# The first 40 microseconds of an attention and FFN block: layer norm's order, its engines, and the queues of the first transfers

## The chip, the cores and the metric

The kernel runs on one core of one Trainium2 chip. Its time is the device time of one execution in microseconds; several executions are taken, and the median counts. A core has five engines that run on their own and meet at semaphores: TensorE (PE, with its weight loads as PEld), VectorE (DVE), ScalarE (ACT), GpSimd (POOL) and SyncE (SP), which here only issues transfers. ACT, POOL and SP can all issue transfers; each works through its instructions in the order of the program.

## The reference

Two sequences of 1024 tokens with 512 features (x is 2 x 1024 x 512, 2048 tokens in all, float32) go through

```python
xn = _layernorm(x)                         # no scale, no shift
s  = attention(xn, w_qkv, b_qkv, w_out, b_out)   # 32 heads of 16, ALiBi, causal softmax
g  = silu(octonion_ffn(xn, w_gate, w_up, w_down)) # weights made ternary: sign times mean |W|
out = x + s * g
```

In the attention, `scores = q k^T / 4 + slope_h * position_k`, masked to the past, softmax, times v, then the output projection. In the FFN each weight is replaced by `scale * clip(round(W / scale), -1, 1)` with `scale = mean |W|` and expanded by the signs of octonion multiplication; `silu(gate) * up` goes through the down weights.

## The kernel before, in words

The tokens are 16 tiles of 128. Eight (the first sequence) are normalised in the head of the kernel, the other eight in the midst of the attention. A tile `t` goes through these steps:

- `measure`: DVE takes mean and variance (`bn_stats`, `bn_aggr`).
- `root`: ACT takes the square root, DVE the reciprocal `rs` and `nb = -mean * rs`.
- `normal`: ACT scales the 128x512 tile in place (`xt`).
- `norm_item`: PE turns the four 128x128 pieces into a PSUM buffer `ptx`, ACT copies them to `xnT` (tokens along the free axis).

In the head `tokens(t)` calls the first three for one tile in a row, so that DVE waits for ACT's root and ACT for DVE's `nb` within each tile.

Heads are worked on in groups of four, and q and k are produced for pairs of groups: `qk_items(b, gp)` are 16 products `pqk` (which of q and k, which half `c` of the tokens, four steps `kt`). A product of 512 columns shows as two PE instructions ("passes"). A finished `pqk` is biased by ACT and DVE into a staging tile `st` of two float32r parts, which SP writes to DRAM (`sp<-st`). `fill_k` and `fill_q` read it back into stacks `k_stack`, `q_stack`, which hold 64 rows of heads, two rows of ALiBi (`al_dram`, made by `alibi_parts`) and two rows for the negated maximum. One half of a stack is four transfers of 128 KB on SP, for k one more from `al_dram`.

Attention runs in 32 units (sequence, group, half of the queries). For each unit PE first makes scores for the row maxima, DVE reduces them (`max_items`), PE and ACT turn the maxima and POOL's queue places them in the q stack (`place_max`, `q_stack<-mr`); then the scores are made again with the maximum in them, ACT takes the exp (`exp_step`, `exp_of`), and PE multiplies by v (`value_step`).

The ternary weights are loaded with three transfers each (`load_weight`: `w_g`, `w_u`, `w_d`). `ternary_sum` is a DVE reduction over such a weight, `ternary_total` a small PE product `tot_g` of the sums, `ternary_signs` two DVE passes, and `keep_signs` writes the signs of the gate and up weights to DRAM.

The order of the instructions on every engine is written out when the program is made, and the engines keep it. For the head it is written by hand or in a list of items (`lead_in`). For the attention a planner in the same function chooses the next item: it keeps a clock `now` with costs per item (436 for a tile's turning, 858 for one q/k step, 431 for one v step, in ns), models of when ACT and DVE will be done, when a filled stack will have landed (`fill_at`, with a step `link` for each fill), and when a weight will be there (`known`). `load_later(w, name)` puts a load of a weight behind a time `known["k", name]` and assumes it landed 9000 later (`known["l", name]`); `weight(name)` then puts sum, total and signs behind that. The items of `later` are taken in the order in which they were put. PSUM buffers are few: three for exp scores, two for maxima, one for the values, and two (`ps_m`) for all the rest, the turned tiles, `pqk`, `pv` and placed maxima among them.

In the kernel before, all eight x tiles are loaded on SP's queue, the first q/k weights (`wqr`) on ACT's beside them, the gate weights on POOL's, the up and down weights and all later `wqr` on ACT's; the 16 x 8 biases of q and k come with eight transfers on SP. The ALiBi table `al_sb` and its low part share the pool of the staging tiles `st`, which has two buffers. 20 products on ones (`idle`, 40 passes) run on PE while nothing else can.

Of the kernel before, what the change touches and what calls it, by code (L numbers as in the profile page):

```python
# [75 lines left out]
def kernel(  # L76
# [108 lines left out]
        )  # L185
        wv_tiles[n] = w

    bqk_sb = aw.tile([P, 2, NP], F32, name="bqk_sb")
    bv_sb = aw.tile([P, D], F32, name="bv_sb")
    mask = aw.tile([P, 512], F32, name="mask")  # L190
    bo_sb = aw.tile([P, D], F32, name="bo_sb")
# [9 lines left out]
    def load_x(t, eng):  # L201
# [3 lines left out]
        eng.dma_start(out=xt, in_=x[t * P : (t + 1) * P, :])  # L205
        x_tiles[t] = xt

    warm = wk.tile([64, 1], F32, tag="rs1", name="warm")
    act_.activation(warm, ones[:, 0:1], AF.Sqrt)
    for t in range(8):  # L210
        load_x(t, sp_)
    load_wq((0, 0), act_)
    load_wv(0)
    for n in range(2):
        for i in range(4):
            sp_.dma_start(
                out=bqk_sb[n * 64 + i * HD : n * 64 + (i + 1) * HD, :, :],
                in_=bqk[i * 32 : i * 32 + HD, :].rearrange(
                    "d (w g n) -> d w g n", w=2, n=2
                )[:, :, :, n],  # L220
            )
    al_sb = stg.tile([P, S], F32, tag="st", name="al_sb")[0:H, :]
    pool_.dma_start(out=al_sb, in_=calibi)
    pool_.dma_start(out=mask, in_=cmask)
    pool_.dma_start(out=bv_sb, in_=bv.partition_broadcast(P))
    add_ring(early, 1, 2)

    xn_tiles = {}
# [9 lines left out]
        dve_.bn_stats(st, x_tiles[t])  # L238
        dve_.bn_aggr(mv[:, t % n, :], st)

    def root(t, n):

        mv = moments[t]
        sd = wk.tile([P, n], F32, tag=f"sd{n}", name=f"sd_{t}")
        act_.activation(sd, mv[:, :, 1], AF.Sqrt, bias=eps)
        rs = wk.tile([P, n], F32, tag=f"rs{n}", name=f"rs_{t}")
        dve_.reciprocal(rs, sd)
        nb = wk.tile([P, n], F32, tag=f"nb{n}", name=f"nb_{t}")
        dve_.scalar_tensor_tensor(nb, mv[:, :, 0], -1.0, rs, ALU.mult, ALU.mult)
        moments[t] = rs, nb  # L250

    def normal(t, n):
        rs, nb = moments[t // n * n]
        i = t % n
        xt = x_tiles.pop(t)
        act_.activation(
            xt, xt, AF.Identity, bias=nb[:, i : i + 1], scale=rs[:, i : i + 1]
        )
        xn_tiles[t] = xt


# [112 lines left out]
    def alibi_parts():  # L374

        for n in range(2):
            home, tag = (stg, "st") if n else (wop, "wo")
            part = home.tile([P, S], F32R, tag=tag, name=f"al_{n}")[0:H, :]
            if n == 0:
                dve_.tensor_copy(part, al_sb)  # L380
                high = part
            else:
                dve_.tensor_tensor(part, al_sb, high.bitcast(F32), ALU.subtract)
            sp_.dma_start(out=al_dram[n], in_=part.bitcast(F32))

    def norm_item(t):
# [64 lines left out]
    def qk_items(b, gp):  # L451

        box = {}

        def product(which, c, kt):
            if (which, c, kt) == (0, 0, 0):
                if (b, gp) not in wq_tiles:
                    compact_wq((b, gp))
                parts[b, gp] = [
                    spill.tile([2, P, S], F32, tag=f"sp{w}", name=f"sp_{b}_{gp}_{w}")  # L460
                    for w in range(2)
                ]
# [3 lines left out]
            pe(  # L466
                nc.tensor.matmul(  # L467
                    ps,
                    lhsT=wq_tiles[b, gp][:, kt, which, :],
                    rhs=xnT[:, kt, b * S + c * 512 : b * S + (c + 1) * 512],  # L470
                    start=(kt == 0),
                    stop=(kt == KD - 1),
                )
            )
            n = b * NP + gp + 1
            if (which, c, kt) == (1, n > 1, KD - 1) and n < B * NP:
                load_wq((n // NP, n % NP), act_)
            if kt < KD - 1:
                return
            bias = bqk_sb[:, which, gp : gp + 1]  # L480
# [353 lines left out]
    def unit_of(lst, n):  # L834
        return lst[n][0] if n < len(lst) else NU
# [78 lines left out]

    def load_later(w, name):
        later(
            lambda: load_weight(w, name, act_),
            lambda: set_known(("l", name), now[0] + 9000),
            ("k", name),
        )  # L920
# [24 lines left out]
    def more_tokens(t0):  # L945

        for t in range(t0, t0 + 4):
            later(
                lambda t=t: measure(t, 4),
                lambda t=t: set_known(("m", t), run_dve(max(now[0], known["x"]), 900)),  # L950
                "x",
            )
            begin[0] += 0.2
        later(
            lambda: root(t0, 4),
            lambda: run_dve(run_act(known["m", t0 + 3], 2800), 350),
        )
# [15 lines left out]
    for n in range(20):  # L973
        pe(nc.tensor.matmul(idle[:, 0:P], lhsT=ones, rhs=ones, start=True, stop=True))
    qk, vs = qk_items(0, 0), v_items(0, 0)
    def tokens(t):
        measure(t, 1)
        root(t, 1)
        normal(t, 1)

    def norm_of(t):
        put([(436, lambda: norm_item(t), "t", ("n", t))])

    make_mask()
    compact_wq((0, 0))
    add_ring(early, 1, 0)
    make_signs()
    load_weight(wg, "g", pool_)
    known.update({("n", t): 7500 + 1600 * t for t in range(8)})
    known.update({("l", "g"): 40000})  # L990
    tokens(0)
    tokens(1)
    for t in range(4):
        norm_of(t)
        quick(lambda t=t: tokens(t + 2))
    put(qk[0:4])
    quick(lambda: (tokens(6), tokens(7), alibi_parts()))
    put(qk[8:12])
    for t in range(4, 8):
        norm_of(t)  # L1000
    put(qk[4:8] + qk[12:16])
    quick(lambda: (begin_v(0, 0), compact_wq((0, 1)), add_ring(early, 2, 3)))
    due = [int(size[0] * n / len(vs)) for n in range(len(vs))]
    lead_in += [(d // 4, None, it) for d, it in zip(due, vs)]
    head_v = len(lead_in)
    lead_in += [(size[0] + 4 * d, None, it) for d, it in zip(due[::2], qk_items(0, 1))]
    known["k", "u"] = 25000
    load_later(wu, "u")
    weight("g")
    later(lambda: keep_signs(0, "g"))  # L1010
# [21 lines left out]
    begin[0] = 10  # L1032
    later(load_wo)
    side = [(d, ok or (lambda: True), it) for d, ok, it in lead_in + side]
    done_qk = [0]

# [9 lines left out]
    SOON = 80  # L1046
    RUN = 1800
    HELD = 1e12
    now, kind = [0.0], ["F"]
    act, dve = [0.0], [0.0]  # L1050
    e_free, x_free, m_free = [0.0] * 3, [0.0] * 2, [0.0] * 2
    o_free = [0.0]
# [18 lines left out]
        dve[0] = max(dve[0], t) + cost  # L1071
        return dve[0]

    qk_done = []

    def try_fill():

        n, part = divmod(fills[0], 4)
        if n >= B * NG or len(qk_done) <= (n // 2 + 1 if n > 1 else part // 2):
            return  # L1080
        if unit_of(exps, E[0]) < 2 * (n - 2) + (0, 1, 2, 2)[part]:
            return
        (fill_q if part % 2 else fill_k)(n // NG, n % NG, part // 2)
        fills[0] += 1
        link[0] = max(now[0], link[0], qk_done[n // 2 + 1 if n > 1 else part // 2]) + 4500
        fill_at.append(link[0] + 2500)

    def try_fetch():
# [114 lines left out]
    def next_side(pos):  # L1203
# [6 lines left out]
        def go():  # L1210
# [345 lines left out]
```

## Time and profile before

| what | value |
|---|---|
| median of 3 runs | 1130.24 us (1127.89 to 1131.73) |
| the profiled execution | 1131.04 us |
| its span, first to last instruction | 1129.2 us |
| mean granted TensorE clock | 0.979 |
| busy: PE / DVE / ACT / POOL | 94% / 61% / 45% / 15% |
| SP's queue: packets, bytes | 66336, 87.48 MB |
| ACT's queue | 3552, 9.78 MB |
| POOL's queue | 3776, 5.98 MB |

A page of the profile gives the busy time of each engine, the span in slices, the DMA queues, and the costliest groups of instructions. A timeline lists instructions in the order of time, merged where the same ones follow each other: start, duration, engine, line, operation, output and inputs, count, and in brackets the idle time of the engine before it with what ended it. "PE ... [3.98 <-ACT xnT]" says that PE did nothing for 3.98 us and that ACT's copy to xnT released it. Names of engines with a q (SPq, ACTq) are of their sequencers, which issue transfers. Line 69 is a helper that issues nearly all instructions of ACT, DVE, POOL and SP, so these go by the tiles' names. The granted clock is the share of full speed that TensorE was given; the records start some 20 us into the span, and a stretch without one is shown as 1.00.

### The profile page before, as it was taken

What the parts mean: (1) busy time and instruction counts of PE and PEld (TensorE: products, weight loads), DVE (VectorE), ACT (ScalarE), POOL (GpSimd) and SP (SyncE); (2) the same over time, 40 slices, a digit from 0 to 9 for tenths busy, and PEclk for the clock granted to TensorE, in tenths of its full rate; (3) what the DMA queues carried; (4) which work ended last, traced back from release to release, by engine and by line L of the source; (5) the groups of instructions that cost most, each with busy time, mean ns of one, the idle gap of its engine ahead of it and who ended that gap; (6) DMA issues with size and microseconds to landing.
All of it is one profiled execution on the core that took longest, in us unless ns stands there. A gap on an engine that the chain in (4) does not pass through costs nothing. (4 is left out here: it accounts for less than half of the span.)

```text
span 1129.2 us, 15583 instructions
## 1 busy us (share of the span) xinstructions
PE 1060.6 (94%) x5562; PEld 700.6 (62%) x5562; DVE 684.5 (61%) x1405; ACT 506.6 (45%) x962; POOL 171.8 (15%) x289
## 2 busy tenths in 40 slices
PE   7879978999999999999999999999899999999995
PEld 5644545675656666556566565665456678878784
DVE  5367786867677777777777867777842114141313
ACT  4122647663844635446445364464583123232322
POOL 6401013010111010100101000001002123242322
PEclk9889979999999999999999999999999999999998
DMA  6886463444735416353442443831131123030110
GB/s 197 202 146 147 99 170 95 67 63 118 151 85 124 101 34 107 135 100 63 122 83 41 103 87 97 139 72 48 43 105 61 47 66 112 1 103 10 58 54 37
DMA packets 73740, 104.24 MB, mean 92 GB/s; under 512 B 26992, under 2 KB 31120, under 8 KB 73664
## 3 DMA queue, kind: packets, MB, share of 16 engines
q1 hardware_dynamic: 66336, 87.48, 34.0%
q10 hardware_dynamic: 3552, 9.78, 2.8%
q0 software_dynamic: 3776, 5.98, 2.1%
q8 instruction: 45, 0.74, 0.3%
q14 instruction: 31, 0.25, 0.1%
HBM read 69.58 MB, written 33.10 MB: 91 GB/s over the span
## 5 line engine op out<-in xcount | busy, mean ns | idle before, releaser
L69 ACT ACTIVATE p<-s 128x512 f32<-128x512 f32 x576 | 310.0, 601 | 125.2 <-PE s L654 70.3
L538 PE MATMUL s<-k_stack,q_stack 126*128 126x512 f32 (+3 forms) x768 | 278.9, 417 | 23.6 <-DVE mx L69 16.1
L654 PE MATMUL s<-q_stack,k_stack 128*128 128x512 f32 (+3 forms) x768 | 229.5, 367 | 13.6 <-DMA q_stack<-mr 8.4
L69 DVE TENSOR_REDUCE mx<-s 128x1 f32<-128x384 f32 (+3 forms) x352 | 226.0, 642 | 11.7
L69 DVE TENSOR_REDUCE left<-s 128x1 f32<-128x512 f32 x256 | 169.1, 685 | 77.0 <-PE s L538 76.0
L538 PEld LDWEIGHTS s<-k_stack,q_stack 126*128 126x128 f32 x768 | 133.1, 194 | 119.0 <-PE s L538 38.4
L654 PEld LDWEIGHTS s<-q_stack,k_stack 128*128 128x128 f32 x768 | 140.3, 193 | 62.2 <-ACT p L69 20.0
L69 DVE TENSOR_TENSOR s<-s,mask 128x128 f32<-128x128 f32 (+2 forms) x352 | 123.9, 352 | 39.4 <-PE s L538 37.7
L692 PE MATMUL po<-p,v 128*32 128x512 f32 (+3 forms) x1536 | 139.0, 490 | 0.3 <-ACT p L69 0.3
L467 PE MATMUL pqk<-xnT,wq 128*128 128x512 f32 x256 | 128.4, 609 | 3.9 <-ACT xnT L69 2.0
L69 DVE SCALAR_TENSOR_TENSOR h<-pu,sc_u,sg 128x512 f32<-128x512 f32 (+1 forms) x44 | 33.0, 750 | 157.9 <-PE pu L1375 153.1
L69 POOL DMA_DIRECT2D q_stack<-mr x64 | 32.1, 507 | 606.5 <-ACT mr L69 606.5
L673 PE MATMUL s<-mask_r,ident_r 128*128 128x256 f32 (+1 forms) x320 | 89.6, 280 | 0.0
L69 POOL TENSOR_TENSOR hs<-h,hs 128x512 fp32r<-128x512 f32 (+1 forms) x43 | 56.2, 1307 | 206.9 <-ACT hs L69 206.9
L692 PEld LDWEIGHTS po<-p,v 128*32 128x32 f32 x1536 | 42.7, 109 | 72.0 <-issue 69.2
L69 ACT ACTIVATE sg<-pg,sc_g 128x512 f32<-128x512 f32 (+1 forms) x44 | 30.4, 691 | 99.7 <-PE pg L1375 99.7
L69 ACT ACTIVATE st<-pqk,bqk_sb 128x512 fp32r<-128x512 f32 x32 | 22.1, 691 | 117.1 <-PE pqk L467 108.7
L425 PE MATMUL pv<-wv,xnT 128*128 128x256 f32 x256 | 68.4, 385 | 1.9 <-DVE v L69 1.5
L467 PEld LDWEIGHTS pqk<-xnT,wq 128*128 128x128 f32 x256 | 47.7, 195 | 31.7 <-issue 21.1
L69 ACT CAST hs<-h 128x512 fp32r<-128x512 f32 (+1 forms) x44 | 27.3, 621 | 85.3 <-DVE h L69 85.3
L673 PEld LDWEIGHTS s<-mask_r,ident_r 128*128 128x128 f32 x320 | 61.3, 192 | 2.1
L761 PE MATMUL pout<-wo_sb,oT 128*128 128x512 f32 x128 | 61.4, 595 | 0.6 <-ACT oT L69 0.6
(145 smaller groups left out, 1103.1 us busy)
## 6 DMA issues: line engine op xcount, KB each, us to landing
sp<-st SPq DMA_DIRECT2D x32, 512.0 KB
k_stack<-sp SPq DMA_DIRECT2D x128, 128.0 KB
q_stack<-sp SPq DMA_DIRECT2D x128, 128.0 KB
wqr<-in_wqk_dram ACTq DMA_DIRECT2D x16, 512.0 KB
xt<-in_x_dram SPq DMA_DIRECT2D x16, 256.0 KB
att<-o SPq DMA_DIRECT2D x32, 128.0 KB
ot<-att SPq DMA_DIRECT2D x16, 256.0 KB
proj<-y SPq DMA_DIRECT2D x16, 256.0 KB
```

The costliest lines, as they stand in the source:

```text
L69: ins = issue(*args, **kwargs)
L425: nc.tensor.matmul(ps[:, 0:256], lhsT=xnT[:, c, b * S + kt * P : b * S + (kt + 1) * P], rhs=wv_tiles[2 * b + hh][:, c, :], start=(c == 0), ...
L467: nc.tensor.matmul(ps, lhsT=wq_tiles[b, gp][:, kt, which, :], rhs=xnT[:, kt, b * S + c * 512 : b * S + (c + 1) * 512], start=(kt == 0), st ...
L538: nc.tensor.matmul(ps[:, j * n : (j + 1) * n], lhsT=q_of(b, g, qc)[0 : NR - 2, first + j, tl * P : (tl + 1) * P], rhs=k_of(b, g, c)[0 : NR ...
L654: nc.tensor.matmul(ps[:, c0 : c0 + w], lhsT=k_of(b, g, kt // 4)[0:NR, h, kt % 4 * P : (kt % 4 + 1) * P], rhs=q[0:NR, h, 512 - w : 512], st ...
L673: pe(nc.tensor.matmul(out, lhsT=ident_r, rhs=rhs, start=False, stop=True))
L692: nc.tensor.matmul(po[32 * i : 32 * i + 32, 512 - w : 512], lhsT=v[:, kt, h * VC : h * VC + 32], rhs=p[:, i * part + c0 : i * part + c0 + ...
L761: nc.tensor.matmul(ps, lhsT=turned[t][:, c, :], rhs=wo_sb[0][:, c, :], start=(c == 0), stop=(c == KD - 1),)
```

## The change

It rewrites the head and the queues that its transfers use:

- Layer norm in the head: `root` is cut in `deviation` (ACT) and `factors` (DVE), and `first_half(t)` takes the moments of tile t and the factors and scaling of tile t - 1. Every second tile (the odd ones) is scaled by POOL (`tensor_scalar`) in place of ACT. The order of the head's steps, with the first eight q/k products, is written out, with two products on ones (`busy(2)`) behind each of the first four turned tiles.
- Transfers: `wqr` of the first pair stands on SP's queue between x tiles 3 and 4; all later `wqr`, the gate, up and down weights go on SP's queue too. `wv`, the 128 columns of the mask that are read, and `bv` follow on SP behind the ALiBi parts. The gate weights leave POOL's queue for a place in the planner (36000 on its clock, the up weights 46000, before 25000).
- Biases of q and k: two transfers on POOL, with the two halves of the partitions shifted by one column, in place of eight on SP.
- The ALiBi table goes to a buffer of the pool of exp results (`pp`), not of the staging tiles.
- The planner starts at HEAD = 21500 with two q/k products done, and its steps for the first group's fills are 3000 in place of 4500.
- POOL's fills of the further stacks and the sign tables come in another order, before the second pair's weights are compacted.

```diff
-    bqk_sb = aw.tile([P, 2, NP], F32, name="bqk_sb")
+    bqk_sb = aw.tile([P, 2 * NG + 1], F32, name="bqk_sb")
...
-    for t in range(8):
+    for t in range(4):
         load_x(t, sp_)
-    load_wq((0, 0), act_)
-    load_wv(0)
+    load_wq((0, 0), sp_)
+    for t in range(4, 8):
+        load_x(t, sp_)
+
+    al = pp.tile([P, 2, S], F32, tag="p", name="al")[0:H]
+    pool_.dma_start(out=al[:, 0], in_=calibi)
+
     for n in range(2):
-        for i in range(4):
-            sp_.dma_start(
-                out=bqk_sb[n * 64 + i * HD : n * 64 + (i + 1) * HD, :, :],
...
-    al_sb = stg.tile([P, S], F32, tag="st", name="al_sb")[0:H, :]
-    pool_.dma_start(out=al_sb, in_=calibi)
-    pool_.dma_start(out=mask, in_=cmask)
-    pool_.dma_start(out=bv_sb, in_=bv.partition_broadcast(P))
+        pool_.dma_start(
+            out=bqk_sb[n * 64 : n * 64 + 64, 1 - n : 1 - n + 2 * NG],
+            in_=bqk.rearrange("(i d) c -> i d c", d=32)[:, 0:HD, :],
+        )
...
-    def normal(t, n):
+    def normal(t, n, on_pool=False):
...
+        if on_pool:
+            pool_.tensor_scalar(
+                xt, xt, rs[:, i : i + 1], nb[:, i : i + 1], ALU.mult, ALU.add
+            )
...
-            if (which, c, kt) == (1, n > 1, KD - 1) and n < B * NP:
-                load_wq((n // NP, n % NP), act_)
+            if (which, c, kt) == (1, 1, KD - 1) and n < B * NP:
+                load_wq((n // NP, n % NP), sp_)
...
     def load_later(w, name):
         later(
-            lambda: load_weight(w, name, act_),
+            lambda: load_weight(w, name, sp_),
...
+    def first_half(t):
+        measure(t, 1)
+        deviation(t, 1)
+        if t % 4:
+            factors(t - 1, 1)
+            normal(t - 1, 1, (t - 1) % 2 == 1)
+
+    for t in range(3):
+        first_half(t)
+    norm_item(0)
+    busy(2)
+    first_half(3)
+    norm_item(1)
+    busy(2)
+    compact_wq((0, 0))
+    factors(3, 1)
+    normal(3, 1, True)
+    for t in (2, 3):
+        norm_item(t)
+        busy(2)
     make_mask()
-    compact_wq((0, 0))
+    alibi_parts()
+    load_wv(0)
+    sp_.dma_start(out=mask[:, 384:512], in_=cmask[:, 384:512])
+    sp_.dma_start(out=bv_sb, in_=bv.partition_broadcast(P))
+    for t in range(4, 7):
+        first_half(t)
+    issue(qk[0:4])
+    norm_item(4)
+    first_half(7)
+    norm_item(5)
+    issue(qk[8:12])
+    factors(7, 1)
+    normal(7, 1, True)
+    norm_item(6)
+    norm_item(7)
     add_ring(early, 1, 0)
+    begin_v(0, 0)
+    add_ring(early, 2, 3)
     make_signs()
-    load_weight(wg, "g", pool_)
-    known.update({("n", t): 7500 + 1600 * t for t in range(8)})
-    known.update({("l", "g"): 40000})
...
     put(qk[4:8] + qk[12:16])
-    quick(lambda: (begin_v(0, 0), compact_wq((0, 1)), add_ring(early, 2, 3)))
+    quick(lambda: compact_wq((0, 1)))
...
-    known["k", "u"] = 25000
+    known["k", "g"] = 36000
+    known["k", "u"] = 46000
+    load_later(wg, "g")
     load_later(wu, "u")
...
-    done_qk = [0]
+    done_qk = [2]
+    HEAD = 21500.0
...
-    now, kind = [0.0], ["F"]
+    now, kind = [HEAD], ["F"]
...
-    qk_done = []
+    qk_done = [HEAD + 4500]
...
+        if n == 0 and now[0] < qk_done[part // 2] - 4000:
+            return
...
-        link[0] = max(...) + 4500
+        link[0] = max(...) + (4500 if n else 3000)
...
-                if done_qk[0] == 2 or done_qk[0] % 4 == 0:
+                if done_qk[0] % 4 == 0:
```

More of the change, by code (lines that the diff above doesn't have):

```diff
@@ L209 @@
     act_.activation(warm, ones[:, 0:1], AF.Sqrt)
-    for t in range(8):
+    for t in range(4):
         load_x(t, sp_)
-    load_wq((0, 0), act_)
-    load_wv(0)
-    for n in range(2):
-        for i in range(4):
-            sp_.dma_start(
-                out=bqk_sb[n * 64 + i * HD : n * 64 + (i + 1) * HD, :, :],
[L218 to L221, printed above, removed]
-    al_sb = stg.tile([P, S], F32, tag="st", name="al_sb")[0:H, :]
-    pool_.dma_start(out=al_sb, in_=calibi)
-    pool_.dma_start(out=mask, in_=cmask)
-    pool_.dma_start(out=bv_sb, in_=bv.partition_broadcast(P))
+    load_wq((0, 0), sp_)
[3 more added lines that the diff above has]
+    pool_.dma_start(out=al[:, 0], in_=calibi)
+    for n in range(2):
+        pool_.dma_start(
+            out=bqk_sb[n * 64 : n * 64 + 64, 1 - n : 1 - n + 2 * NG],
+            in_=bqk.rearrange("(i d) c -> i d c", d=32)[:, 0:HD, :],
+        )
     add_ring(early, 1, 2)
@@ L239, in measure, with deviation @@
         dve_.bn_aggr(mv[:, t % n, :], st)
-    def root(t, n):
+    def deviation(t, n):
         mv = moments[t]
@@ L245, in root, with factors @@
         act_.activation(sd, mv[:, :, 1], AF.Sqrt, bias=eps)
+        moments[t] = mv, sd
+    def factors(t, n):
+        mv, sd = moments[t]
         rs = wk.tile([P, n], F32, tag=f"rs{n}", name=f"rs_{t}")
@@ L255, in normal @@
         xt = x_tiles.pop(t)
-        act_.activation(
-            xt, xt, AF.Identity, bias=nb[:, i : i + 1], scale=rs[:, i : i + 1]
-        )
+        if on_pool:
+            pool_.tensor_scalar(
+                xt, xt, rs[:, i : i + 1], nb[:, i : i + 1], ALU.mult, ALU.add
+            )
+        else:
+            act_.activation(
+                xt, xt, AF.Identity, bias=nb[:, i : i + 1], scale=rs[:, i : i + 1]
+            )
         xn_tiles[t] = xt
@@ L376, in alibi_parts @@
         for n in range(2):
-            home, tag = (stg, "st") if n else (wop, "wo")
-            part = home.tile([P, S], F32R, tag=tag, name=f"al_{n}")[0:H, :]
             if n == 0:
-                dve_.tensor_copy(part, al_sb)
+                part = wop.tile([P, S], F32R, tag="wo", name="al_high")[0:H, :]
+                dve_.tensor_copy(part, al[:, 0])
                 high = part
             else:
-                dve_.tensor_tensor(part, al_sb, high.bitcast(F32), ALU.subtract)
+                part = al[:, 1].bitcast(F32R)
+                dve_.tensor_tensor(part, al[:, 0], high.bitcast(F32), ALU.subtract)
             sp_.dma_start(out=al_dram[n], in_=part.bitcast(F32))
@@ L475, in product @@
             n = b * NP + gp + 1
-            if (which, c, kt) == (1, n > 1, KD - 1) and n < B * NP:
-                load_wq((n // NP, n % NP), act_)
+            if (which, c, kt) == (1, 1, KD - 1) and n < B * NP:
+                load_wq((n // NP, n % NP), sp_)
             if kt < KD - 1:
                 return
-            bias = bqk_sb[:, which, gp : gp + 1]
+            bias = bqk_sb[:, 1 + 2 * (which * NP + gp) :][:, 0:1]
             st = stg.tile([P, 2, 512], F32R, tag="st", name=f"st_{b}_{gp}_{which}_{c}")
@@ L954, in more_tokens @@
         later(
-            lambda: root(t0, 4),
+            lambda: (deviation(t0, 4), factors(t0, 4)),
             lambda: run_dve(run_act(known["m", t0 + 3], 2800), 350),
@@ L975, with busy, issue @@
     qk, vs = qk_items(0, 0), v_items(0, 0)
-    def tokens(t):
-        measure(t, 1)
[L978 to L982, printed above, removed]
-    make_mask()
-    compact_wq((0, 0))
+    def busy(n):
+        for _ in range(n):
+            pe(nc.tensor.matmul(idle[:, 0:P], lhsT=ones, rhs=ones, start=True, stop=True))
+    def issue(items):
+        for _, emit, _ in items:
+            emit()
+    def first_half(t):
+        measure(t, 1)
+        deviation(t, 1)
[15 more added lines that the diff above has]
+        busy(2)
+    make_mask()
+    alibi_parts()
[13 more added lines that the diff above has]
+    norm_item(7)
     add_ring(early, 1, 0)
+    begin_v(0, 0)
+    add_ring(early, 2, 3)
     make_signs()
-    load_weight(wg, "g", pool_)
-    known.update({("n", t): 7500 + 1600 * t for t in range(8)})
-    known.update({("l", "g"): 40000})
[L991 to L1000, printed above, removed]
     put(qk[4:8] + qk[12:16])
-    quick(lambda: (begin_v(0, 0), compact_wq((0, 1)), add_ring(early, 2, 3)))
+    quick(lambda: compact_wq((0, 1)))
     due = [int(size[0] * n / len(vs)) for n in range(len(vs))]
@@ L1084, in try_fill @@
         fills[0] += 1
-        link[0] = max(now[0], link[0], qk_done[n // 2 + 1 if n > 1 else part // 2]) + 4500
+        link[0] = max(now[0], link[0], qk_done[n // 2 + 1 if n > 1 else part // 2]) + (4500 if n else 3000)
         fill_at.append(link[0] + 2500)
```

## The prediction

> **What bounds the kernel now.** I read the page first, then busy time by stretches, then the timelines of PE, DVE, ACT and SyncE over the first 160 us, then SP's own waits.
>
> The page, sections 1 and 2:
>
> ```profile
> span 1129.2 us, 15583 instructions
> PE 1060.6 (94%) x5562; PEld 700.6 (62%) x5562; DVE 684.5 (61%) x1405; ACT 506.6 (45%) x962; POOL 171.8 (15%) x289
> ```
>
> TensorE sets the end: 68.6 us of the span are its idle time, and whatever the change gives must come out of these, or out of PE work that brings nothing (the 40 passes on "ones", 8.9 us), or out of work done at half clock. The profiled execution took 1131.0 us (span 1129.2 and 1.8 around it), 0.8 over the median of 1130.24; sums are made against 1131.0 and the 0.8 is taken off at the end.
>
> PE's timeline (start, duration, line, what, count, the idle time before it and who ended it), cut to the head:
>
> ```profile
> 1.08 8.90 PE L974 MATMUL idle<-ones 64*128 64x128 f32 x40 [1.08 <-DVE ones L69]
> 9.90 1.97 PE L391 MATMUL ptx<-ident,xt 128*128 128x128 f32 x8
> ...
> 17.51 8.52 PE L467 MATMUL pqk<-xnT,wq 128*128 128x512 f32 x16 [1.35 <-ACT xnT L69]
> ...
> 30.45 2.80 PE L391 MATMUL ptx<-ident,xt 128*128 128x128 f32 x12 [3.98 <-ACT xnT L69]
> 33.92 8.86 PE L467 MATMUL pqk<-xnT,wq 128*128 128x512 f32 x16 [0.68 <-ACT xnT L69]
> 42.62 7.61 PE L425 MATMUL pv<-wv,xnT 128*128 128x256 f32 x34
> ...
> 57.19 0.38 PE L320 MATMUL tot_g<-wsum_g,ones 64*128 64x1 f32 x2
> ...
> 78.93 0.76 PE L654 MATMUL s<-q_stack,k_stack 128*128 128x512 f32 x1 [3.88 <-DMA q_stack<-mr]
> ```
>
> Two waits stand out: 3.98 us in the head, and 3.88 us ahead of the first exp scores. The cause of the first is on ACT: the second staging tile `st` shared its pool with `al_sb`, and DVE's alibi work came late.
>
> ```profile
> 29.23 0.69 ACT L69 ACTIVATE st<-pqk,bqk_sb 128x512 fp32r<-128x512 f32 x1 [1.07 <-DVE al L69]
> ```
>
> From 42.8 to 78.9 PE was idle 6.2 us (1.54 + 0.41 + 0.33 + 3.88 in its timeline). SyncE's queue in that stretch, and DVE's first use of the gate weights:
>
> ```profile
> 48.37 1.73 SPq L69 DMA_DIRECT2D k_stack<-sp  x4
> ...
> 52.41 2.85 SPq L69 DMA_DIRECT2D k_stack<-sp  x4
> 56.98 3.30 SPq L69 DMA_DIRECT2D q_stack<-sp  x4
> 60.98 3.27 SPq L69 DMA_DIRECT2D k_stack<-sp  x4
> 64.99 0.23 SPq L69 DMA_DIRECT2D k_stack<-al_dram  x1
> 65.95 3.30 SPq L69 DMA_DIRECT2D q_stack<-sp  x4
> 55.26 1.55 DVE L69 TENSOR_REDUCE wsum_g<-w_g 64x1 f32<-64x1360 f32 x1
> ```
>
> Each fill of a quarter stack (128 KB) takes 1.0 us of this queue, because an issue waits for earlier fills to land (SP's waits name k_stack and q_stack DMAs for 15.8 us). From the first fill of half 1 (48.37) to the last of group 1 (68.95) are 20.6 us, and whatever stands behind in SyncE's queue waits for all of them. `w_g` didn't: it went out on GpSimd's queue at 17.1.
>
> **The change, part by part.**
>
> Layer norm of tiles 0 to 3. DVE still starts at 5.44 behind its two memsets; the staggered order has tile 0 scaled at about 8.4 (0.69 + 0.18 and 0.30 for the root, one more stats pair before the factors, 0.82 scaling). But PE's "ones" end only at 9.98. From there PE does four times a tile's transposes (1.97/2 = 0.98) and `busy(2)` (4 passes of 8.90/40 = 0.22, so 0.89): 9.98 + 4 x 1.87 = 17.5. Before, the first pqk started at 17.51: the gain of the staggering is eaten by the 3.6 us of `busy`. GpSimd's scaling isn't in the trace: its 128x128 copies take 0.29, the 128x2048 casts 1.89, its 128x512 two-input subtractions 1.31, so 0.6 to 1.3; I take 0.8, nearer the one-input rows. At either end tile 1 is ready at 9.9 at the latest and wanted at 11.9, so it costs nothing; without that cover it would be 0.5.
>
> [...] In this trace 40 passes in a row over 8.9 us stayed at 222 ns each, while the 512-column pqk passes fell from 0.85 to 0.43 us some 2.8 us after they began. [...]
>
> Tiles 4 to 7 and the rest of q and k. The alibi tile leaves the staging pool, so the 3.98 wait goes. From 17.5: 16 pqk passes 8.5; four tiles of transposes at full clock (0.60 each, the row of the `pm` transposes) 2.4; two waits of 0.9 for a PSUM buffer (ACT 0.69 + DVE 0.75, less a tile's transposes); the last copy 0.7; 16 pqk passes at 0.427, 6.85, since the gap that halved the clock at 30 is gone. End 37.8 instead of 42.8: **-5.0**. [...]
>
> The bias: two DMAs on GpSimd in place of eight on SyncE (6.1 us of that queue, waited for by nobody). `wv`, mask and `bv` move behind the alibi on SyncE, wanted at 38 and later, on the queue by 15: nothing.
>
> First scores. The planner starts its clock at HEAD = 21.5 and puts the first fills at 22.4; with link steps of 3.0 the scores are due at 34.5, behind 15 pv items (30 passes; 17 items before). On the chip: 37.8 + 30 x 0.224 = 44.5 instead of 49.9. The 11 maxima of unit 0 took DVE from 50.66 to 69.3; less the gate weights (4.5) and its idle time (2) that is 12 us, so 56.8, and the maxima are placed some 12 us sooner.
>
> The gate weights. Their load goes from GpSimd at 17 to SyncE, at 36.1 on the planner's clock. All eight fill groups have been put on the queue by 32, and 1 MB of `wqr` now stands among them as well. The planner believes in landing 9 us later (45.1) and, behind the load of `w_u` at 46.1, puts the sum on DVE, and `tot_g` on PE behind it at 49, ahead of the first exp scores (51.5). On the chip: the second half of k is staged by 39.2 (37.8 + 0.69 + 0.75), its spill took 4.0 before (44.32 to 48.37), `wqr` adds 1 MB at some 400 GB/s (the best window of the DMA view shows 418), 2.6; so half 1's fills start at 45.8 to 48. Plus 20.6, plus 1.0 for the issue, plus landing: 4.1 unloaded (w_g's own median), 7.2 loaded (the rows of maxima at 71). That is 71.5 to 77; taken 75, as the queue is full. The sum takes 1.55: `tot_g` at 73 to 78.6, taken 77. PE reaches `tot_g` at about 60 (56.8, and four q/k items of 0.9 less what overlaps). Queued behind it on PE are the exp scores of unit 0, whose maxima have been in place for long; behind the sum on DVE are the maxima of unit 1 and the bias steps, so PE can do nothing else. **PE idles 17 us (13 to 18.6)** where it idled 6.2: **+10.8**.
>
> Counted the other way: at about 79 PE stands where it stood, but with 14 passes of q/k for the next pair (0.45 each, 6.3) and three maxima (0.9) undone that had been done: +7.2 less 2 for the earlier start. Both ways give +5 to +6.
>
> [...]
>
> Later. `wqr` and `w_d` off ACT's queue: 0.82 x 6 and 1.81 us of ACT; PE's wait for ACT behind w_d was 1.1: -1.0 (0 to -4). `w_d` behind k fills on SyncE (140.8 to 143.2) lands some 4 to 5 us later than at 145, and DVE wants it at 148.2: +1.5 (0 to 3). The signs of g are now kept late, and a p buffer waits for it: +0.5 (0 to 3). The planner reorders everything behind: 0, give or take 3, from its idle of 2 to 5 us per 100 us later on.
>
> Sum: -5.0 + 10.8 - 1.0 + 1.5 + 0.5 = +6.8; less 0.8 for the median: **1137.0 us**.
>
> **Rivals.**
>
> 1. The gate weights come in time (the fills run faster, or the sum stands further back): then the head keeps -5.0, most of the old 6.2 idle goes with 4.5 us of DVE work out of the first maxima, and the half-clock stretch behind 78 (windows 70:80 and 80:90 show 0.92 and 0.74) gives 2. That is -9 to -13: 1117 to 1121. It decides from a landing before about 69 (idle below 11.2). For it: four fills at 43 to 46 landed in under 1 us each. Against: 1.0 us a fill from 52 to 69. Chance 0.27, with part of it near 1125.
> 2. Balance: landing near 69 to 71, 1127 to 1133. Chance 0.10.
> 3. The clock also falls in the head, or `w_u`, queued behind `w_g`, holds the spills of the next pair: +3 to +7 on top, 1140 to 1146. Counted among the slower, 0.63 in all.
> 4. The change doesn't shorten the head at all (pqk at half clock through): +2 at most, within case 3.
>
> **Numbers.** Slower 0.63 with 1137 as its middle and 1134 to 1146 as its own range; no measurable change (0.3%, 3.4 us, about what can be told here) 0.10; faster 0.27. The 8 in 10 reach from 1120, into the first rival, to 1146.
>
> **What would show it.** Right: SP issues `w_g` behind the last q_stack fill of group 1, past 64; DVE's `wsum_g` waits over 10 us for that DMA; PE's wait before `tot_g` is its longest of the run; pqk of pair 0 ends near 38; first pqk near 17.5. Wrong: `w_g` lands before 66, or the exp scores of unit 0 run ahead of `tot_g`; then rival 1. [...]

## The result and the profile after

The changed kernel takes 1138.65 us (median, 1138.3 to 1139.78) against 1130.99 for the kernel before in the same comparison: ratio 1.0074, 95% interval 1.0051 to 1.0096. It is slower, by 0.7%. The profiled execution took 1138.8 us; section 1 of its page, with the engines' busy time, has the span:

```profile
span 1137.0 us, 15603 instructions
PE 1064.8 (94%) x5578; PEld 702.1 (62%) x5578; DVE 683.6 (60%) x1405; ACT 502.1 (44%) x958; POOL 174.5 (15%) x290
```

PE is busy 4.2 us more and idle 3.6 us more (72.2 against 68.6). That alone tells little, because PE's busy time holds half-clock work (the mean granted clock of the span is 0.975, against 0.979 before). PE's timeline of the first 112 us tells more (start, duration, line, what, count, in brackets the idle time before it and what ended it):

```profile
1.08 8.90 PE L983 MATMUL idle<-ones 64*128 64x128 f32 x40 [1.08 <-DVE ones L69]
9.91 1.12 PE L400 MATMUL ptx<-ident,xt 128*128 128x128 f32 x4
10.96 1.22 PE L989 MATMUL idle<-ones 64*128 64x128 f32 x4
...
18.71 5.35 PE L476 MATMUL pqk<-xnT,wq 128*128 128x512 f32 x8
...
32.17 1.02 PE L400 MATMUL ptx<-ident,xt 128*128 128x128 f32 x4 [2.26 <-POOL xt L69]
33.87 9.73 PE L476 MATMUL pqk<-xnT,wq 128*128 128x512 f32 x16 [0.68 <-ACT xnT L69]
...
49.84 1.04 PE L547 MATMUL s<-k_stack,q_stack 126*128 126x128 f32 x6
...
79.79 0.55 PE L329 MATMUL tot_g<-wsum_g,ones 64*128 64x1 f32 x2 [13.74 <-DVE wsum_g L69]
...
85.62 1.42 PE L663 MATMUL s<-q_stack,k_stack 128*128 128x512 f32 x1
...
111.10 2.08 PE L476 MATMUL pqk<-xnT,wq 128*128 128x512 f32 x2 [3.69 <-POOL wq L69]
```

Three places are to be seen. The head isn't shorter: the products of the first pair end at 43.6 (33.87 + 9.73), where they ended at 42.8. Then PE stands 13.74 us in front of `tot_g`, and the first exp scores start at 85.62, where they started at 78.93. And a new wait of 3.69 us stands at 111, for the weights of the third pair.

The stall is DVE's, and DVE's is a transfer's. DVE's timeline, and SyncE's of the same stretch (its duration is that of issuing, with what an issue waits for):

```profile
78.08 1.56 DVE L69 TENSOR_REDUCE wsum_g<-w_g 64x1 f32<-64x1360 f32 x1 [14.31 <-DMA w_g<-in_wg_dram]
```

```profile
50.51 1.73 SPq L69 DMA_DIRECT2D k_stack<-sp  x4
...
66.56 2.88 SPq L69 DMA_DIRECT2D q_stack<-sp  x4
70.07 2.29 SPq L69 DMA_DIRECT2D w_g<-in_wg_dram  x3
```

The gate weights go out at 70.07, behind the last fill of the second group, and are in place at 78; before, the same sum ran at 55.26. In the windows view (stretch, length, busy time and count of PE, PEld, DVE, ACT, POOL, then the granted clock, DMA share and GB/s) hardly anything but DMA works from 70 to 80 (DVE's sum begins at 78.08), and the granted clock is 0.50:

```profile
70.00:80.00 10.00, 0.21 (x2) 0.24 (x2) 1.92 (x2) 0.00 (x0) 0.00 (x0) 0.50 1.10 177
80.00:90.00 10.00, 8.79 (x29) 5.80 (x30) 6.24 (x11) 2.55 (x5) 0.00 (x0) 0.65 0.61 143
```

How far the changed kernel is behind can be followed at the 576 exps on ACT, numbered in order: the first is 7.3 us later than in the kernel before, the 13th 12.5, the 37th 11.0, the 85th 11.9, the 349th 8.1, the last 8.3. All of the loss is made before the 13th exp. Two things stand behind the 5.2 us from the first to the 13th. The planner of the changed kernel puts fewer products of the next pair ahead of the first exp scores: PE has 12 `pqk` passes between the first pair and these scores, where it had 22, and 42 instead of 32 from there to the 13th exp, ten passes of 0.43 us or some 4.3 us. And PE is idle 2.2 us more there (4.8 against 2.6), above all for the third pair's weights, 3.69 us against 0.94; the line of the kernel before is

```profile
99.68 1.98 PE L467 MATMUL pqk<-xnT,wq 128*128 128x512 f32 x4 [0.94 <-POOL wq L69]
```

A 3.4 us stretch at half clock follows the 3.69, but half clock is no loss here: in all, the changed kernel has 4.7 us of it between the first exp scores and the 13th exp, the kernel before 6.3. Of the 2.8 us given back between the 252nd and the 349th exp (10.9 behind at the 252nd), 1.7 are a further half-clock stretch of 3.4 us that the kernel before had at 553 and the changed one doesn't; the rest stays open.

### The profile page after: what moved, and what is told of

Same layout as the page of the kernel before. It is cut to its first block, busy times and chain, and to the rows that moved or that the text cites. A ratio compares the mean times of both kernels' runs of the same rounds, so it can differ in the third digit from the quotient of the medians.

```text
span 1137.0 us, 15603 instructions
## 1 busy us (share of the span) xinstructions
PE 1064.8 (94%) x5578; PEld 702.1 (62%) x5578; DVE 683.6 (60%) x1405; ACT 502.1 (44%) x958; POOL 174.5 (15%) x290
## 5 line engine op out<-in xcount | busy, mean ns | idle before, releaser
L547 PEld LDWEIGHTS s<-k_stack,q_stack 126*128 126x128 f32 x768 | 132.3, 192 | 123.7 <-PE s L547 40.5
L476 PE MATMUL pqk<-xnT,wq 128*128 128x512 f32 x256 | 133.4, 627 | 5.8 <-POOL wq L69 3.7
```

Of the source, the lines that this page charges most:

```text
L476: nc.tensor.matmul(ps, lhsT=wq_tiles[b, gp][:, kt, which, :], rhs=xnT[:, kt, b * S + c * 512 : b * S + (c + 1) * 512], start=(kt == 0), st ...
L547: nc.tensor.matmul(ps[:, j * n : (j + 1) * n], lhsT=q_of(b, g, qc)[0 : NR - 2, first + j, tl * P : (tl + 1) * P], rhs=k_of(b, g, c)[0 : NR ...
```

## The experiments

My theory was: (a) the loss is the order on PE and DVE in front of a load that lands at 78, and the load is late because SyncE's queue takes its transfers in turn (`w_g` at 70.07, behind fills from 50.51 on); (b) the head's gain is missing because tile 7 is scaled too late; whatever (b) gives back, the stall eats. Rivals: the stall only shows a loss that would come anyway (the fills, or the placed maxima, set the time), and the loss lies in GpSimd's scaling or in the passes on ones.

**The gate weights alone go back to GpSimd's queue** (the order on PE, DVE and ACT stays).

```diff
     make_mask()
+    load_weight(wg, "g", pool_)
...
-    load_later(wg, "g")
+    later(lambda: None, lambda: set_known(("l", "g"), now[0] + 9000), ("k", "g"))
```

> Only the queue of the gate weights' load changes: from SyncE, behind all fills, to GpSimd, right behind the masks (about 16 us); the planner's clock and the order on PE, DVE and ACT stay. Theory (the wait for w_g behind the fills is the loss): DVE's wait before wsum_g and PE's wait before tot_g fall from 14.3 and 13.7 to under 1.5 us, the first exp scores start at 72 to 75 instead of 85.6, now held by the placed maxima (the q_stack<-mr transfer), and the kernel takes 1125 to 1129. Rival (PE has nothing to do in that stretch anyway, the wait only changes its name): first exp scores at 82 or later, 1135 to 1139.

Measured: 1128.36 us, ratio to the kernel before 0.9979 (0.9968 to 0.999). This one transfer's queue is worth 10.3 us of the changed kernel. PE's timeline shows what is late next, the maxima placed in the q stack:

```profile
72.12 0.47 PE L663 MATMUL s<-q_stack,k_stack 128*128 128x512 f32 x1 [2.22 <-DMA q_stack<-mr]
```

The first exp comes 7.2 us before that of the kernel before, the 13th 0.6 after it. In between PE has 42 `pqk` passes here too, ten more than the kernel before, and it waits 3.81 us for the third pair's weights:

```profile
98.99 1.12 PE L476 MATMUL pqk<-xnT,wq 128*128 128x512 f32 x2 [3.81 <-POOL wq L69]
```

So the undone passes and the wait at 111 belong to the change too, and not to the gate weights.

**The converse: in the kernel before, the gate weights alone move to SyncE's queue**, behind the planner's clock.

```diff
-    load_weight(wg, "g", pool_)
-    known.update({("l", "g"): 40000})
...
+    known["k", "g"] = 31000
+    later(lambda: load_weight(wg, "g", sp_), lambda: set_known(("l", "g"), now[0] + 9000), ("k", "g"))
```

> The kernel before with one thing of the change alone: the gate weights are loaded on SyncE's queue at 31 on the planner's clock (behind all fills) instead of on GpSimd's at 17 us; the planner still believes them there at 40, so the order on PE, DVE and ACT stays. Theory: w_g lands at 75 to 79, PE waits 15 to 21 us before tot_g, and the kernel takes 1140 to 1147. Rival (a load's queue is of no matter, 9 us are enough): 1129 to 1132, no wait before tot_g over 2.

Measured: 1150.13 us, ratio 1.0169 (1.0147 to 1.019). The same move costs 19 us here, 3 more than the upper end of the theory. PE's timeline:

```profile
79.03 0.58 PE L320 MATMUL tot_g<-wsum_g,ones 64*128 64x1 f32 x2 [20.19 <-DVE v L69]
```

The releaser named is DVE's `v`; DVE's own longest wait is the 20.1 us of `wsum_g` for `w_g` (it starts at 77.09, inside the 75 to 79 expected), and `v` stands behind it. Here products of v and 22 `pqk` passes stood behind the stall, and the first exp scores start only at 99.64.

**The queue stays, only the planner's belief changes:** the changed kernel, with `w_g` at its place behind the same fills, but taken to land 29 us after its issue in place of 9.

```diff
-            lambda: set_known(("l", name), now[0] + 9000),
+            lambda: set_known(("l", name), now[0] + (29000 if name == "g" else 9000)),
```

> The changed kernel with one number altered: the planner is told that the gate weights land 29 us after their issue on its clock, not 9. They stay on SyncE's queue, at the same place behind the same fills; only their sum, tot_g and signs are placed further back on DVE and PE (tot_g stands behind 11 exp-score items of unit 0 and the first values). My theory (the price is the order on DVE and PE, which trust a landing that the queue can't keep, not the transfer's late arrival in itself): tot_g's wait falls from 13.7 us to below 2, the first exp scores come near 72 as in the kernel with w_g on GpSimd's queue, and the time is 1127 to 1131, most of the 10 us of that kernel. Rival (a load that arrives at 78 costs anyway: the signs come late, and the later loads behind it hold up the next pair): 1134 to 1139.

Measured: 1132.34 us, ratio 1.0017 (1.0003 to 1.0031), between the two expectations. The stall is gone: `tot_g` waits 1.39 us, at 94, and the exp scores start at 71.70. So 6.3 of the 10.3 us come back by the order alone; the changed kernel's order trusted a landing which the queue couldn't keep. What is left shows in PE's and SyncE's timelines:

```profile
71.70 0.77 PE L663 MATMUL s<-q_stack,k_stack 128*128 128x512 f32 x1 [3.63 <-DMA q_stack<-mr]
...
94.03 0.38 PE L329 MATMUL tot_g<-wsum_g,ones 64*128 64x1 f32 x2 [1.39 <-DVE st L69]
...
105.63 4.37 PE L476 MATMUL pqk<-xnT,wq 128*128 128x512 f32 x6 [7.97 <-POOL wq L69]
```

```profile
88.47 5.89 SPq L69 DMA_DIRECT2D sp<-st  x2
97.52 0.49 SPq L69 DMA_DIRECT2D signs_dram<-w_g  x1
98.11 1.63 SPq L69 DMA_DIRECT2D wqr<-in_wqk_dram  x2
```

The signs of g are ready on DVE at 97.49 (95.86 + 1.63); their transfer waits for them, and the weights of the third pair stand behind it on SyncE's queue, which did nothing else from 94.36 (88.47 + 5.89) on. PE waits 7.97 us for these, 4.2 more than with `w_g` on GpSimd's queue. That the rest is this second place in the queue is read from the timelines; no run took it away by itself.

**The head: the factors of tile 7 go ahead of the second staging.**

```diff
     norm_item(5)
-    issue(qk[8:12])
     factors(7, 1)
     normal(7, 1, True)
+    issue(qk[8:12])
```

> Only factors and scaling of tile 7 move ahead of the four products of qk[8:12], so that DVE takes them ahead of the second staging step. Theory: the 2.26 us wait of PE for tile 7 and the half clock from 32.4 to 39.2 go, pqk of pair 0 ends near 39 instead of 43.5, but the wait before tot_g eats most of it, since w_g still stands behind the fills, which start only some 2 to 4 us sooner: 1134.5 to 1137, with a wait before tot_g of 14 to 17. Rival (the head is where the change lost its time): the whole 4.5 us come through, 1133 to 1134, with the wait before tot_g unchanged at 13.7.

Measured: 1138.66 us, ratio 1.0063 (1.0043 to 1.0083): the changed kernel's time, above both expectations. PE's timeline shows gain and loss:

```profile
33.32 7.13 PE L476 MATMUL pqk<-xnT,wq 128*128 128x512 f32 x16 [0.68 <-ACT xnT L69]
...
79.15 0.55 PE L329 MATMUL tot_g<-wsum_g,ones 64*128 64x1 f32 x2 [16.09 <-DVE wsum_g L69]
```

The products run at full clock now (1.00 in the windows view from 33 to 41, where the changed kernel had 0.50 from 33 to 39) and end 3.2 us sooner, at 40.4; the wait in front of `tot_g` is 2.35 longer. The head's gain isn't an accident of one execution: the first pair ends at 42.7 to 43.6 in the three profiles with the changed kernel's order of tile 7, and at 39.0 to 40.5 in the six with the factors moved and the passes on ones kept. A head that ends sooner only waits longer for the same landing.

**Both edits together.**

> Both edits. Theory: with w_g there, the head's gain passes to the first exp scores as far as the fills let it: they start at 68 to 73, and the kernel takes 1121 to 1127, 1 to 5 below the run with w_g alone. Rival (fills and the placing of the maxima set the first exp scores, the head doesn't): within 1 of the run with w_g alone.

Measured: 1126.15 us, ratio 0.9957 (0.9942 to 0.9972). With the stall gone, the head's 2.8 us (40.4 against 43.2 in the run with `w_g` alone) are worth 2.2 by the medians, though the two intervals just overlap. The first exp scores start only 0.4 sooner: POOL's queue issues the placed maxima 1.8 us sooner (62.58 against 64.36), but the last of them lands at 71.60 against 71.98, and PE's wait for them is 3.87 us instead of 2.22.

```profile
71.73 0.47 PE L663 MATMUL s<-q_stack,k_stack 128*128 128x512 f32 x1 [3.87 <-DMA q_stack<-mr]
```

**Without the passes on ones** (both edits kept, the three lines with `busy(2)` taken out, which are 16 passes).

> On top of the run with both edits: without the eight products on ones behind the first turned tiles. Theory (they don't release the clock, only full windows of 512-column passes did): the first pqk starts near 16 instead of 18.7, now held by tile 3's scaling; its passes still run at 0.85 us for about the first 3.4 us behind it; pqk of pair 0 ends 1.5 to 3 sooner than 40.3, and the kernel takes 1124 to 1126.5, as the placed maxima hold the first exps. Rival (they keep the array warm): first pqk passes stay at 0.85 us for 6 us or more and the clock falls again in the head, pair 0 ends at 41 or later, 1127 to 1130.

Measured: 1127.22 us, ratio 0.9972 (0.9958 to 0.9987): no better, and 0.7 us above the theory's range, in that of the rival. The rival's mechanism doesn't show, though: the pair ends sooner, and its last 16 passes take 7.13 us, 0.43 each, to the end of the head. PE's timeline:

```profile
16.02 5.58 PE L476 MATMUL pqk<-xnT,wq 128*128 128x512 f32 x8 [0.67 <-ACT xnT L69]
...
29.65 7.13 PE L476 MATMUL pqk<-xnT,wq 128*128 128x512 f32 x16 [0.68 <-ACT xnT L69]
...
58.14 0.76 PE L547 MATMUL s<-k_stack,q_stack 126*128 126x512 f32 x1 [2.90 <-DMA q_stack<-sp]
```

The products end at 36.8, 3.6 us sooner than with the ones. The fills of half 1 begin only 1.6 us sooner (47.80 against 49.41), PE waits 2.90 for one of them, and its 512-column passes are slow behind that wait (0.76 us for the one at 58.14, 0.47 for the one at 53.91) and again behind the next one (0.77 at 71.48). The passes on ones cost the head their full time, and the products behind them run no faster for it (the first eight passes take 6.51 us with them, 5.58 without), yet the time they cost is free here: the fills and the placed maxima set the pace. What it is that raises the clock in the head, no run here shows.

**Every scaling on ACT** (both edits kept).

```diff
-            normal(t - 1, 1, (t - 1) % 2 == 1)
+            normal(t - 1, 1)
```

and the same for tiles 3 and 7.

> On top of the run with both edits: all eight tiles are scaled by ACT, none by GpSimd. Theory (PE's ones and turned tiles are the path of the first four tiles, and POOL's 1.13 us scaling of tile 3 ends at 14.2, 2.3 us ahead of its use): first pqk at 18.7 as before, pair 0's end within 0.7 of 40.3, and 1125 to 1127.5. Rival (the scaling on GpSimd is what lets the head run): tile 3 late, first pqk at 20 or later, 1128 or more.

Measured: 1124.60 us, ratio 0.9954 (0.9939 to 0.9968), against 0.9957 with GpSimd. The first product starts at 18.68 (18.70), the pair ends at 40.2 (40.4). GpSimd's share neither helps nor hurts.

**The ALiBi table alone** (with its low part), moved out of the staging pool in the kernel before.

```diff
-    al_sb = stg.tile([P, S], F32, tag="st", name="al_sb")[0:H, :]
+    al = pp.tile([P, 2, S], F32, tag="p", name="al")[0:H]
```

> The kernel before with the ALiBi table alone moved to the exp pool. The prediction laid PE's 3.98 us wait in the head to the shared staging pool: by that it goes whole, pair 0 ends near 38 and the time falls by up to 5, to 1125 to 1127. Rival, from the order on ACT (the roots and scalings of tiles 6 and 7 stand ahead of the second staging step and end at 28.2): only the 1.07 us of ACT's wait for the ALiBi goes, PE's wait is 2.6 to 3.2, the clock still falls near 31, 1129 to 1131.

Measured: 1128.51 us, ratio 0.9989 (0.9969 to 1.0008): no difference that can be told, 0.5 us below the rival's range. PE's wait of 3.98 us at 30 becomes 2.96, not 0, as the rival had it, and the first pair still ends at 42.7:

```profile
29.91 1.09 PE L391 MATMUL ptx<-ident,xt 128*128 128x128 f32 x8 [2.96 <-ACT xnT L69]
```

ACT still takes the second staging only at 28.69, right behind the scaling of tile 7:

```profile
27.82 0.81 ACT L69 ACTIVATE xt<-xt,nb,rs 128x512 f32<-128x512 f32 x1 [0.42 <-DVE nb L69]
...
28.69 0.69 ACT L69 ACTIVATE st<-pqk,bqk_sb 128x512 fp32r<-128x512 f32 x1
```

The buffer was the last of two waits, and the order on ACT stood 1 us behind it.

**The third pair's weights sooner** (with both edits): later `wqr` are issued at the end of the q products instead of the k products.

```diff
-            if (which, c, kt) == (1, 1, KD - 1) and n < B * NP:
+            if (which, c, kt) == (int(n == 1), 1, KD - 1) and n < B * NP:
```

> On top of the run with both edits: the weights wqr of a later pair are loaded at the end of the running pair's q products, eight products sooner, still on SyncE's queue. Theory (of what eats the sooner first exps: pair 2's products stand at the head of PE's queue and wait for a load that only goes out when pair 1's last product is done): PE's wait for POOL's wq near 98 (3.5 us) falls under 0.5, the half clock behind it (99.6 to 103) goes, and the kernel takes 1120 to 1123.5. Rival (unit 1's maxima on DVE set the pace there, PE only waits in another place): 1125 to 1127.

Measured: 1124.44 us, ratio 0.9948 (0.993 to 0.9966), between the two expectations, and not to be told from the 0.9957 of the run without this edit. The wait for `wq` falls from 3.46 to 1.08 us; 1.50 of it comes back at once for placed maxima:

```profile
96.39 1.12 PE L476 MATMUL pqk<-xnT,wq 128*128 128x512 f32 x2 [1.08 <-POOL wq L69]
...
112.05 0.93 PE L663 MATMUL s<-q_stack,k_stack 128*128 128x512 f32 x3 [1.50 <-DMA q_stack<-mr]
```

**The same kernel on another occasion, and beside it the one with every scaling on ACT added.**

> The kernel with w_g on GpSimd, the factors of tile 7 earlier and the later pairs' q/k weights loaded at the end of the q products, on the same chip as the one with all scalings on ACT added: 1124.4 as before if the chip doesn't matter; the difference between the two is what GpSimd's scalings cost (theory: 0 to 1.5 us).

> Four edits on the changed kernel together: w_g on GpSimd's queue at 20, the factors of tile 7 ahead of the second staging, the later pairs' q/k weights at the end of the q products, and every scaling on ACT instead of every second on GpSimd. If the parts add up: 1124.4 and 1124.6 with three of the four each, against 1126.2 without the last two, so 1122 to 1123.5. Rival (behind 71 the placed maxima hold the first exp scores whatever the head does, and the third edit only moved its wait): 1124 to 1126.

Measured: 1121.53 us, ratio 0.9929 (0.9911 to 0.9946), and with the scalings on ACT 1122.35, ratio 0.9932 (0.9915 to 0.9949). The second lies where adding up the parts had put it, but not for that reason: the kernel without its last edit was 2.9 us faster than the 1124.4 of the first occasion (the intervals overlap), and against that the scalings on ACT bring nothing. In the two profiles the first exp scores start at 68.47 and at 71.35, both behind `q_stack<-mr`; the transfers varied. With GpSimd's scalings kept, it is the fastest version found, 0.5 to 0.7% faster than the kernel before, and its parts are the change's own, with one load, one step and one trigger in other places.

## Why the prediction came out as it did

The direction and the main cause were right; that the time, 1137.0 against 1138.65, came out so close is in part luck. In the two profiled executions 7.8 us were lost, where the sum had 6.8. The head lost 0.8 instead of giving 5.0. The idle time behind it cost 8.7 instead of 10.8. By the 13th exp the kernel was 12.5 us behind, 3.0 of them in no term. Then 4.7 came back, where the later terms had another 1.0 of loss.

Of the signs that were to show it right, three came (the issue of `w_g` past 64, DVE's wait of over 10 us, PE's longest wait in front of `tot_g`) and two didn't: the first pair ended at 43.6, not near 38, and the first product started at 18.71, not near 17.5.

**The landing of the gate weights.** Right in its cause, and somewhat late in its time. The load was put behind the last q_stack fill, past 64; it is issued at 70.07. It was to land at 71.5 to 77, taken 75; it landed at 78. The fills behind half 1's staging began at 50.51, not at 45.8 to 48, in part because the head wasn't shorter: with the head mended they begin at 48.75. They took 18.9 us (50.51 to 69.44), and 20.9 by the same count in the kernel before (48.37 to 69.25). That the load waits for all the fills ahead of it in SyncE's queue was right, and the two runs with only its queue changed show what that costs: 10.3 us in one kernel, 19 in the other; issuing the load took SyncE 2.29 us (at 70.07). The run with the sum placed later adds that 6.3 of the 10.3 are paid only because the engines' order trusted an earlier landing.

**PE's idle time in front of `tot_g`.** Taken as 17 (13 to 18.6), measured 13.74 and another 1.2 behind it for the scale. It was smaller because PE came to it at 66, not at 60, as the head ended 5.8 us later than predicted (43.6 against 37.8), while `tot_g` ran only 2.8 us later than the 77 taken. With the head mended it is 16.09, near the value taken. The term "+10.8" was +8.7 (13.74 + 1.2 - 6.2).

**The head, -5.0: the step that failed.** It measured +0.8 (43.6 against 42.8). Three of its parts were wrong.

First, the 3.98 us were laid to the staging buffer alone. With that buffer freed and nothing else changed, 2.96 remain: ACT's order, tiles 6 and 7 in front of the second staging, set nearly the same time. A wait that a view puts down to one releaser may hide another one just behind it.
Second, in the changed order DVE's factors of tile 7 stand behind the second staging step. DVE's and POOL's timelines show the chain that I had not followed:

```profile
30.23 0.75 DVE L69 SCALAR_TENSOR_TENSOR st<-pqk,bqk_sb,st 128x512 fp32r<-128x512 f32 x1 [3.60 <-ACT st L69]
30.90 0.15 DVE L69 RECIPROCAL rs<-sd 128x1 f32<-128x1 f32 x1
```

```profile
31.35 0.77 POOL L69 TENSOR_SCALAR xt<-xt,rs,nb 128x512 f32<-128x512 f32 x1 [10.49 <-DVE nb L69]
```

The reciprocal runs the moment that the staging step is through; tile 7 is scaled at 31.35, PE waits 2.26 for it, and behind that wait the granted clock is half from 32.3 to 39.1, so that 16 passes take 9.73 us instead of 7.13. The windows view (PEclk, the granted clock, stands ahead of the last two numbers):

```profile
33.00:39.00 6.00, 5.32 (x7) 2.19 (x7) 0.00 (x0) 0.59 (x1) 5.83 (x4) 0.50 0.76 135
```

The prediction had a clock that also falls in the head among its rivals and did not take it into its sum; the run with the factors moved shows 3.2 for wait and clock together, 2.6 of them (9.73 - 7.13) the clock.
Third, the first product started at 18.71, not at 17.5: a tile's turning with its four passes on ones takes 2.2 us ((18.71 - 9.91) / 4), not 1.87: by the rows the turning takes 1.12 and not 0.98, and the four passes 1.22 and not 0.89, with little overlap.

**`busy` and the clock.** Right by the row (by their starts the passes on ones are 213 to 215 ns apart to the end; the prediction's 222 is 8.90/40). PE worked from 1.08 to 18.7 on ones and turned tiles, and in this profile the 512-column passes still ran at 0.85 us until 22.2. Why they did, no run here shows.

**GpSimd's scaling at nothing.** Right: 0.76 to 0.77 us an instruction and once 1.13 (0.8 taken), and no gain that can be told with all of them on ACT.

**The later terms.** `wqr` and `w_d` off ACT, -1.0: between the 13th and the 37th exp the lag falls by 1.5, but no run shows that this is why. `w_d` behind the k fills, +1.5: not seen; PE waits 1.32 us at `tot_d`, where it waited 1.33. Not in the sum at all: the third pair's weights at 111, 2.75 us more waiting. The ten undone passes stand only in the prediction's second count, as 14. The prediction looked at what the weights of pairs do to others on SyncE's queue, not at who waits for them.

**The rivals.** "The gate weights come in time" was put at 1117 to 1121; with them in time the kernel takes 1128.36, and with the head mended as well 1126.15. The mechanism was right, but its gain was too large, since it stacked the whole head on top of the removed stall and did not ask what is late next: the placed maxima, then `wq`. Its support, "four fills at 43 to 46" that landed fast, isn't in the rows: one fill is issued there, at 43.23, the next four from 48.37 on, and no row shows when SyncE's fills land.

Of the third and fourth rivals the conditions came true: the clock fell in the head, and the head was no shorter. The 3 to 7 us that the third put on top did not come. A head that ends later only shortens the wait in front of `tot_g`; the run with the factors moved, which is without that loss, takes the same 1138.66 us.

## What to carry to other kernels

Here a load that moved to another queue was issued behind all that stood in that queue (`w_g` at 70.07, behind fills from 50.51 on), and what the engines' written order put behind its first use waited too (PE for 13.74 us): work out the landing from the queue's own rows, and place the first use by that, or leave the load on a queue that has nothing to wait for. Time gained in front of a fixed landing was only longer waiting (the head 3.2 us shorter, the wait 2.35 longer, the kernel's time the same), so remove the latest wait first and count an earlier stage's gain only up to the next one. When a wait has one named releaser, look at which instruction on its engine would have run next without it, because two causes can stand a microsecond apart, as here (of 3.98 us, 2.96 remained).

## What the runs showed of the hardware

- In the head the 512-column passes were slow at first. In the changed kernel's profile they start 0.853 us apart from 19.7 on and 0.43 apart from 22.2 on (the first one starts at 18.71); in the kernel before the same change of pace comes at 20.7, with the first at 17.51. In the nine profiles of the changed kernel and its variants that show the head, the first eight passes take 5.08 to 6.55 us and the next eight 3.60. The 40 passes on ones ahead of them, 64 rows and 8.9 us, start 213 to 215 ns apart to the end, but for the first pair; that is a quarter of the 0.853 us. A turned tile takes 1.12 us at 9.91 to 16.51, and 0.60 at 23.90. Without `busy`, the products began 2.7 us sooner (16.02 against 18.70), and their first eight passes took 5.58 us instead of 6.51.
- In the profiles of the kernel before and of the changed one the stretches of half clock, the one at the end of the span apart, last 3.4 us (two in each), 6.8 (three before, two after), 10.2 (one in each) and 17.1 (one after). Behind the same 2.26 us wait for tile 7 the 16 passes took 9.73 us in the changed kernel and 9.55 with `w_g` on GpSimd's queue, and the first pair ended at 43.6 and 43.2; with the factors moved they took 7.13.
- GpSimd's `tensor_scalar` with two per-partition operands on 128x512 float32 takes 0.76 to 0.77 us, and 1.13 to 1.14 for the one at 13.03 or 13.04, in all four profiles whose GpSimd rows show it.
- In the idle stretch of 13.74 us on PE the granted clock fell to half at 69.9 and stayed there to 86.9, 7 us beyond the end of the stretch at 79.8; in the same profile shorter gaps of 2.26 and 3.69 us each had a stretch of half clock behind them, of 6.8 and 3.4 us.
